# A second recursion level for five of seven block products in a fused layer kernel, with a leftover pass moved ahead

## The chip, the core and the metric

The kernel runs on one core of a Trainium2 chip. The metric is device time in microseconds, the median of several runs. The core has five engines with a queue each, and every queue is worked strictly in order: TensorE (PE, matmuls into the accumulator memory PSUM), VectorE (DVE), ScalarE (ACT), GpSimd (POOL) and SyncE (SP, which here issues all DMAs). An instruction that has to wait for another engine waits on a semaphore, and everything behind it in its own queue waits with it. SBUF is the on-chip working memory; PSUM has eight banks of 512 fp32 columns for each of 128 partitions.

## What is computed

A transformer layer on 2048 tokens of width 512: layer norm, linear attention and a feed-forward network with low-rank expert terms, both added to the input. The part that matters here, cut to its core:

```
gate = x @ W_gate + _lora(x, sA_gate, sB_gate, scale) + _expert_lora(x, A_gate, B_gate, w, scale)
up   = x @ W_up   + _lora(x, sA_up, sB_up, scale)     + _expert_lora(x, A_up, B_up, w, scale)
hidden = jax.nn.silu(gate) * up
out = hidden @ W_down + ...
```

`gate` and `up` have 1376 features each: ten chunks of 128, and 96 left over. All numbers are fp32.

## The kernel before, in words

Tokens are handled in two batches `b` of 1024. After the norm, the normalized input stands transposed in SBUF (`xnT[b]`, two tiles of 256 input features). Features are handled in five pairs `j` of chunks (`j` and `j + 5`), which makes ten *units* (j, b), in the order (0,0), (0,1), (1,0) and so on to (4,1).

In a unit, the product "weights times input" is split into 2x2 blocks: two chunks of features, two blocks of 512 tokens, two halves of the input width. Seven products of block sums (a Strassen scheme in Winograd's form) replace eight. The block sums of tokens are `tsum[b][p]`, those of weights are the eight slots `A11, A12, S1, S3, S2, S4, A21, A22` of a tile for gate and one for up (`wsum[j]`). Each product exists twice (m = 0 for gate, m = 1 for up), and has two matmuls of 512 columns for each: a *wide* product has four matmuls.

Three of the seven products (1, 6 and 5) are done in the units of `unit2` with the same scheme once more: the 2x2 blocks are now gate and up against two halves of the width and two halves of 256 tokens. Such an *inner* product (`inner`, a generator with four steps) has seven matmuls of 256 columns in place of four of 512. It uses one PSUM tile `ab` with two halves `ua` and `lo`, and half of a tile `x` which products 1 and 6 share. ScalarE copies `ua` into the result tiles `r`, VectorE adds `x` and `lo` to them. The inner sums of weights are made by `inner_weight_sums(j)` (VectorE, four instructions of 384 columns for products 1, 5 and 6), those of tokens by `inner_token_sums(b)`. The two units with j = 0 (`unit`) do all seven products wide; `fold`, `attend`, and the inner sums run in between as hooks.

The order on each engine is the order in which the program is written, except on SP. A unit of `unit2` issues: step 1 of product 1; the low-rank terms (`low_rank`, on 64 rows each, gate and up in pairs); half of product 2; then the steps of products 1, 6 and 5 interleaved with the wide matmuls of 2 and 7; then product 3 wide, low-rank terms, product 4 wide. Each of the four output blocks (0,0), (1,1), (0,1), (1,0) is closed by two adds on VectorE and handed to `gated`: Silu on ScalarE, and later (at the next `flush`) a multiplication on VectorE and a store by SP into `h_dram`.

In the b = 0 unit, hooks `mid` and `late` fold a shared low-rank term into the next pair's weights (four small matmuls into four PSUM banks, then four adds on VectorE: `fold_pe`, `fold_adds`), and `end` makes the eight weight sums of the first level (`fold_sums`). In the b = 1 unit, the hook `sums` makes the inner weight sums for the next pair. In the units PSUM has four rotating banks (`bank`) and four held ones (`held`).

The 96 left-over features have their own passes: `rest_weights` loads their weights (and makes a small table on POOL), `fold_rest` adds the shared low-rank term, `rest(b)` does the matmuls for a batch, with Silu, copy, multiplication and a store into `r_dram`. In the kernel before, `rest_weights` stands at j = 2, `fold_rest` in unit (4,0), `rest(0)` between (4,0) and (4,1), and `rest(1)` after (4,1), with the fold of the last down-projection weights in its middle.

Ahead of the units, `query_unit(0)` and `query_unit(1)` make the attention's queries, with hooks for other work; `attend(b, g)` divides them. After the units comes the output stage (`emit_unit`), four blocks of down-projection which read the stored hidden features back (`load_feature`, `feature_sums`). Its tiles come from the slots that the units leave free (`RING`).

Of the kernel before, what the change touches and what calls it, by code (L numbers as in the profile page):

```python
# [9 lines left out]
F32 = mybir.dt.float32  # L10
# [4 lines left out]
P = 128  # L15
# [3 lines left out]
DIV_EPS = 1e-8  # L19

# [15 lines left out]
def layer_kernel(  # L36
# [162 lines left out]
    spread = ffn.tile([P, 2, P], F32, name="spread")  # L199
# [266 lines left out]
    ws = {}  # L466
# [65 lines left out]
    bdiff = ffn.tile([2 * ER, P], F32, name="bdiff")  # L532
# [228 lines left out]
    nc.gpsimd.tensor_sub(bdiff, bgu_sb[:, 0:P], bgu_sb[:, NP * P : (NP + 1) * P])  # L761

    def fold(j, i):
# [5 lines left out]

    query_unit(1, {  # L770
        "P1": [lambda: attend(0, 0)],
        "P5": [lambda: attend(0, 1)],
        "P3": [fold(0, 0)],
    })
    load_weights(1)
    low_rank_in(2)
    low_rank_in(3)
    fold(0, 1)()
    denominators(1)

    def u_tile(name):
        return up_.tile([P, TB], F32, tag="u", name=name)

    def gated(gate, up, m, tag, store):
        h = hp.tile([P, TB], F32, tag="h", name=f"h{tag}")
        nc.scalar.activation(h[0:m, :], gate[0:m, :], AF.Silu)  # L786

        def rest():
            nc.vector.tensor_mul(h[0:m, :], h[0:m, :], up[0:m, :])
            store(h)  # L790

        later(rest)

    def unit(j, b, hooks):

        ws = wsum[j][0]
        tag = f"{j}_{b}"
        f1, f2 = ts(j, P), ts(j + NP, P)
        blk = [ts(0, TB), ts(1, TB)]
        ps = {}  # L800
        c = {}

        def low_rank(terms):
            for p, w, cols, g in terms:
                for m in range(2):
                    ps[m, p] = bank(f"p{p}{m}_{tag}")
                    rows = slice(m * ER, (m + 1) * ER)
                    nc.tensor.matmul(ps[m, p], w[rows, cols], xa[b][rows, blk[g]], start=True, stop=False)

        def products(p):  # L810
            for m in range(2):
                first = (m, p) not in ps
                if first:
                    ps[m, p] = bank(f"p{p}{m}_{tag}")
                for k in range(2):
                    nc.tensor.matmul(  # L816
                        ps[m, p], ws[m][:, A_OF[p], ts(k, P)], tsum[b][p][:, k, :],
                        start=first and k == 0, stop=(k == 1),
                    )
            return ps[0, p], ps[1, p]  # L820

        def gate(half, g):
            def store(h):
                nc.sync.dma_start(
                    out=h_dram[b][j][:, :, 2 * half + g, :].rearrange("s p n -> p s n"),
                    in_=h.rearrange("p (s n) -> p s n", n=UT),
                )

            gated(c[0, half, g], c[1, half, g], P, f"{half}{g}_{tag}", store)

        def hook(name):
            for f in hooks.get(name, ()):
                f()

        low_rank([(2, bgu_sb, f1, 0), (5, bgu_sb, f2, 1)])
        u = [u_tile(f"u{m}_{tag}") for m in range(2)]
        u4 = [u_tile(f"v{m}_{tag}") for m in range(2)]
        pp = products(1)
        for m in range(2):
            nc.scalar.copy(u[m], pp[m])  # L840
        hook("P1")
        pp = products(2)
        for m in range(2):
            c[m, 0, 0] = u_tile(f"c11{m}_{tag}")
            nc.vector.tensor_add(c[m, 0, 0], u[m], pp[m])
        flush()
        gate(0, 0)
        hook("P2")
        pp = products(6)
        for m in range(2):  # L850
            nc.vector.tensor_add(u[m], u[m], pp[m])
        hook("P6")
        pp = products(5)
        for m in range(2):
            nc.vector.tensor_add(u4[m], u[m], pp[m])
        flush()
        hook("P5")
        pp = products(7)
        for m in range(2):
            c[m, 1, 1] = u_tile(f"c22{m}_{tag}")  # L860
            nc.vector.tensor_add(c[m, 1, 1], u4[m], pp[m])
            nc.vector.tensor_add(u[m], u[m], pp[m])
        gate(1, 1)
        hook("P7")
        low_rank([(3, bdiff, f1, 1), (4, bgu_sb, f2, 0)])
        pp = products(3)
        for m in range(2):
            nc.vector.tensor_add(u4[m], u4[m], pp[m])
            c[m, 0, 1] = u4[m]
        flush()  # L870
        gate(0, 1)
        pp = products(4)
        for m in range(2):
            nc.vector.tensor_add(u[m], u[m], pp[m])
            c[m, 1, 0] = u[m]
        flush()
        gate(1, 0)


    TI = {}  # L880
    TH = TB // 2

    def inner_token_sums(b):

        both = slot(7 if b == 0 else 4, [2, 4, TH], f"ti56_{b}")
        if b == 0:
            ti1.append(slot(6, [NBATCH, 4, TH], "ti1"))
        t12 = tsum_pair[b]
        for src, to in ((t12, both), (xnT[b][0][:, :, 0:TB].unsqueeze(1), ti1[0][:, b : b + 1])):
            b11, b12 = src[:, :, 0, 0:TH], src[:, :, 0, TH:TB]  # L890
            b21, b22 = src[:, :, 1, 0:TH], src[:, :, 1, TH:TB]
            nc.vector.tensor_sub(to[:, :, 0], b12, b11)
            nc.vector.tensor_sub(to[:, :, 1], b22, to[:, :, 0])
            nc.vector.tensor_sub(to[:, :, 2], b22, b12)
            nc.vector.tensor_sub(to[:, :, 3], b21, to[:, :, 1])
        for p, t in ((1, ti1[0][:, b]), (5, both[:, 0]), (6, both[:, 1])):
            raw = tsum[b][p]
            TI[b, p] = {1: raw[:, 0, 0:TH], 2: raw[:, 1, 0:TH], 3: raw[:, 1, TH:TB],
                        4: t[:, 3], 5: t[:, 0], 6: t[:, 1], 7: t[:, 2]}

    ti1 = []
    WI = {}

    def inner_weight_sums(j):

        wi = slot(5, [4, 4, P], f"wi{j}")[:, 0:3]
        g, u = (t[:, 0:6:2, :].rearrange("p s (k m) -> p s k m", m=P) for t in wsum[j][0])
        nc.vector.tensor_add(wi[:, :, 0], u[:, :, 0], u[:, :, 1])
        nc.vector.tensor_sub(wi[:, :, 1], wi[:, :, 0], g[:, :, 0])
        nc.vector.tensor_sub(wi[:, :, 2], g[:, :, 0], u[:, :, 0])  # L910
        nc.vector.tensor_sub(wi[:, :, 3], g[:, :, 1], wi[:, :, 1])
        for i, p in enumerate((1, 5, 6)):
            WI[p] = {1: g[:, i, 0], 2: g[:, i, 1], 3: wi[:, i, 3], 4: u[:, i, 1],
                     5: wi[:, i, 0], 6: wi[:, i, 1], 7: wi[:, i, 2]}

    def held(name, k):
        return ps_held[0].tile([P, TB], F32, tag=f"held{k}", name=name)

    def inner(p, b, tag):

        r = [u_tile(f"r{p}{m}_{tag}") for m in range(2)]
        s0, s1 = slice(0, TH), slice(TH, TB)
        ab = bank(f"ab{p}_{tag}", [P, 2, TH])
        ua, lo = ab[:, 0], ab[:, 1]

        def mm(out, n, start=False):
            nc.tensor.matmul(out, WI[p][n], TI[b, p][n], start=start, stop=True, skip_group_check=True)  # L927


        mm(ua, 1, start=True)  # L930
        nc.scalar.copy(r[0][:, s0], ua)  # L931
        x_ = xbank(p, tag)
        mm(x_, 2, start=(p != 6))
        nc.vector.tensor_add(r[0][:, s0], r[0][:, s0], x_)  # L934
        yield r

        mm(lo, 7)
        mm(ua, 6)
        nc.scalar.copy(r[1][:, s0], ua)
        yield r  # L940
        mm(ua, 5)
        nc.scalar.copy(r[1][:, s1], ua)
        nc.vector.tensor_add(r[1][:, s1], r[1][:, s1], lo)
        yield r
        mm(lo, 4)
        mm(ua, 3)
        nc.scalar.copy(r[0][:, s1], ua)  # L947
        nc.vector.tensor_add(r[1][:, s0], r[1][:, s0], lo)  # L948
        yield r

    xs = {}

    def xbank(p, tag):

        if p == 1:
            xs[tag] = bank(f"x_{tag}", [P, 2, TH])
        return xs[tag][:, 1 if p == 6 else 0]

    def unit2(j, b, mid=(), late=(), end=(), sums=()):

        ws = wsum[j][0]
        tag = f"{j}_{b}"
        f1, f2 = ts(j, P), ts(j + NP, P)
        x0, x1 = xa[b][:, 0:TB], xa[b][:, TB:BT]
        c = {}

        def low_rank(terms, start):
            for banks, cols, act in terms:
                for m in range(2):
                    rows = slice(m * ER, (m + 1) * ER)  # L970
                    nc.tensor.matmul(  # L971
                        banks[m], bgu_sb[rows, cols], act[rows, :], start=start, stop=True, skip_group_check=True
                    )
# [483 lines left out]
```

## Time and profile before

| what | value |
|---|---|
| median of 3 runs | 755.51 us (754.02 to 756.65) |
| the profiled run | 756.13 us |
| its span in the profile | 754.3 us |
| mean granted TensorE clock | 1.00 |

Where the stages lie on TensorE, and the busy time of the engines in each (us, read from the profile's table of windows):

| stretch | what | PE | DVE | ACT | POOL |
|---|---|---|---|---|---|
| 221.5 to 283.4 | units (0,0), (0,1) | 61.15 | 47.50 | 8.66 | 3.46 |
| 283.4 to 312.1 | unit (1,0) | 28.67 | 15.19 | 6.14 | 0 |
| 312.1 to 339.1 | unit (1,1) | 27.00 | 18.87 | 6.82 | 0 |
| 339.1 to 478 | units (2,0) to (4,0) | 138.90 | 82.97 | 33.49 | 0 |
| 478 to 492 | `rest(0)` | 14.00 | 3.33 | 3.54 | 0 |
| 492 to 521 | unit (4,1) | 29.00 | 17.10 | 7.91 | 5.87 |
| 521 to 535.5 | `rest(1)` and the last folds | 14.28 | 12.52 | 2.98 | 11.91 |
| 535.5 to the end | output stage | | | | |

The profile is one execution. Its rows show the line, the engine, the operation, the tiles (out<-in), the shape and the count; a timeline row starts with the start time and the length in us, and the bracket at its end is the idle time before it and what ended it. TensorE passes over each fp32 matmul twice, so each matmul of the program shows as two records.

### The profile page before, as it was taken

The numbers are of one execution on the slowest core, as the hardware profiler recorded it, in microseconds if no ns is written. First come the engines' busy times: TensorE is split into PE (matmuls) and PEld (weight loads), VectorE is DVE, ScalarE is ACT, GpSimd is POOL, SyncE is SP. The second block draws the span as 40 slices with busy tenths as digits, with TensorE's granted clock in tenths as the row PEclk, the third lists the DMA queues.
The fourth block names the chain that finished last, engine by engine and source line by source line (L and its number), as shares of the span: only waits on it lengthen the run. The fifth ranks groups of instructions, "written<-read, shape, count | busy, mean of one in ns | idle before, by whom it ended". The sixth has DMA issues, their size and how long they took to land.

```text
span 754.3 us, 8036 instructions
## 1 busy us (share of the span) xinstructions
PE 743.8 (99%) x2950; PEld 467.6 (62%) x2950; DVE 403.7 (54%) x857; ACT 166.5 (22%) x332; POOL 80.7 (11%) x126
## 2 busy tenths in 40 slices
PE   8999999999999999999999999999999999999997
PEld 7666666454343436456456556463688888888886
DVE  5666665455686683774674674439722602603303
ACT  3544442533331112222122122231100000000000
POOL 3111212011000100000000000006601002201001
PEclk9999999999999999999999999999999999999999
DMA  8811001006322212112112122327604407313001
GB/s 223 218 46 43 15 0 57 0 1 167 113 53 70 83 39 77 60 46 67 56 59 73 38 73 77 124 89 204 203 33 175 143 15 234 126 53 115 29 1 56
DMA packets 52729, 63.24 MB, mean 84 GB/s; under 512 B 9426, under 2 KB 39506, under 8 KB 52435
## 3 DMA queue, kind: packets, MB, share of 16 engines
q1 hardware_dynamic: 52018, 62.46, 26.5%
q8 instruction: 23, 0.38, 0.2%
q10 hardware_dynamic: 672, 0.28, 0.2%
q14 instruction: 16, 0.12, 0.1%
HBM read 40.97 MB, written 21.76 MB: 83 GB/s over the span
## 4 chain that ended last, share of the span: by engine, by line
PE 95%; ACT 2%; DVE 2%; issue 0%; DMA 0%; POOL 0%; DVEq 0%; ACTq 0%
PE po L1314 25%; PE ab L927 8%; PE b L977 8%; PE pk L274 7%; PE p L816 7%; PE pg L302 6%; PE x L977 4%; PE p L977 4%; PE pqu L555 3%; PE ph L1337 3%; PE pqv L555 2%; PE pr L1107 2%; PE pxa L634 2%; PE b L971 2%; PE x L927 1%; PE x L971 1%
## 5 line engine op out<-in xcount | busy, mean ns | idle before, releaser
L1314 PE MATMUL po<-wd,f 128*128 128x256 f32 x560 | 122.4, 380 | 0.2 <-DVE xr L1383 0.2
L1314 PEld LDWEIGHTS po<-wd,f 128*128 128x128 f32 x560 | 106.0, 190 | 16.8 <-issue 2.4
L274 PE MATMUL pk<-wk_sb,xnT 128*128 128x256 f32 (+1 forms) x256 | 61.9, 396 | 1.1 <-ACT xnT L262 1.1
L977 PE MATMUL b<-t,w 128*128 128x512 f32 x128 | 61.0, 603 | 0.0
L302 PE MATMUL pg<-kt,xn 128*128 128x512 f32 x128 | 57.5, 592 | 0.0
L274 PEld LDWEIGHTS pk<-wk_sb,xnT 128*128 128x128 f32 x256 | 49.0, 197 | 9.3 <-ACT xnT L262 1.9
L1344 DVE TENSOR_TENSOR had<-ph,wT 64x256 f32<-64x256 f32 x8 | 3.4, 422 | 90.7 <-PE ph L1337 90.6
L1314 PE MATMUL po<-kvo,f 128*128 128x256 f32 x224 | 49.4, 381 | 0.0
L1314 PEld LDWEIGHTS po<-kvo,f 128*128 128x128 f32 x224 | 42.3, 190 | 7.1 <-issue 1.5
L1361 ACT COPY a<-po 128x512 f32<-128x512 f32 x4 | 2.3, 585 | 199.1 <-PE po L1314 159.0
L302 PEld LDWEIGHTS pg<-kt,xn 128*128 128x128 f32 x128 | 24.4, 190 | 25.2 <-issue 23.7
L977 PEld LDWEIGHTS b<-t,w 128*128 128x128 f32 x128 | 23.3, 190 | 25.5 <-issue 24.2
L927 PE MATMUL ab<-ti,wi 128*128 128x256 f32 x144 | 37.6, 379 | 0.0
L927 PEld LDWEIGHTS ab<-ti,wi 128*128 128x128 f32 x144 | 27.0, 190 | 10.9 <-ACT r L931 4.2
L1129 POOL TENSOR_TENSOR wd<-wd 128x256 f32<-128x256 f32 x5 | 3.8, 760 | 269.6 <-issue 267.2
L948 DVE TENSOR_TENSOR r<-r,ab 128x256 f32<-128x256 f32 x24 | 10.1, 419 | 40.3 <-ACT r L947 40.3
L977 PE MATMUL x<-xnT,w 128*128 128x512 f32 x64 | 30.9, 605 | 0.0
L934 DVE TENSOR_TENSOR r<-r,x 128x256 f32<-128x256 f32 x24 | 10.0, 418 | 36.6 <-PE x L927 25.5
L977 PE MATMUL p<-xnT,w 128*128 128x512 f32 x64 | 28.8, 592 | 0.0
L816 PE MATMUL p<-t,w 128*128 128x512 f32 x64 | 28.8, 597 | 0.0
L300 POOL TENSOR_TENSOR ksum<-ksum,kt 128x512 f32<-128x512 f32 x14 | 19.9, 1422 | 78.4 <-DVE kt L292 47.8
L786 ACT ACTIVATE h<-c 128x512 f32<-128x512 f32 x20 | 12.6, 630 | 58.7 <-DVE c L995 29.1
(250 smaller groups left out, 1146.1 us busy)
## 6 DMA issues: line engine op xcount, KB each, us to landing
h_dram<-h SPq DMA_DIRECT2D x40, 256.0 KB
f<-h_dram SPq DMA_DIRECT2D x20, 512.0 KB
x_ring<-in_x_dram SPq DMA_DIRECT2D x16, 256.0 KB
q_dram<-qt SPq DMA_DIRECT2D x16, 256.0 KB
f<-q_dram SPq DMA_DIRECT2D x8, 512.0 KB
xr<-in_x_dram SPq DMA_DIRECT2D x8, 512.0 KB
out_dram<-xr SPq DMA_DIRECT2D x16, 256.0 KB
w<-in_w_gate_dram SPq DMA_DIRECT2D x10, 256.0 KB
```

The source lines that it names most:

```text
L274: nc.tensor.matmul(pk[s], xt(i // TPBATCH, c, cols), wk_sb[:, c, s * HD : (s + 1) * HD + s * E], start=(c == 0), stop=(c == NC - 1),)
L300: nc.gpsimd.tensor_add(ksum, ksum, kt)
L302: nc.tensor.matmul(pg[m], xn[:, ts(m, P)], kt, start=(j == 0), stop=(j == TPBATCH - 1))
L555: nc.tensor.matmul(banks[c], wqs[p][:, k, ts(c, P)], tsum[b][p][:, k, :], start=(start and k == 0), stop=(k == 1), skip_group_check=True,)
L634: nc.tensor.matmul(pa, agu_sb[:, c, :], xt(b, c, cols), start=(c == 0), stop=(c == NC - 1))
L816: nc.tensor.matmul(ps[m, p], ws[m][:, A_OF[p], ts(k, P)], tsum[b][p][:, k, :], start=first and k == 0, stop=(k == 1),)
L927: nc.tensor.matmul(out, WI[p][n], TI[b, p][n], start=start, stop=True, skip_group_check=True)
L971: nc.tensor.matmul(banks[m], bgu_sb[rows, cols], act[rows, :], start=start, stop=True, skip_group_check=True)
L977: nc.tensor.matmul(banks[m], ws[m][:, A_OF[p], ts(k, P)], tsum[b][p][:, k, :], start=start and k == 0, stop=True, skip_group_check=True,)
L1107: nc.tensor.matmul(ps, t[:, k, 0:P], xt(b, k, blk[g]), start=False, stop=(k == NC - 1))
L1314: nc.tensor.matmul(ps[p][:, q, :], lhsT, rhs, start=start, stop=stop, skip_group_check=True)
L1337: nc.tensor.matmul(ph[g * ER : (g + 1) * ER, :], a, f[:, g, :], start=(n == 0), stop=(n == len(chunks) - 1), skip_group_check=True,)
```

## The change

1. All ten units are now of one kind, `unit`, in which five products (1, 2, 6, 5, 3) are inner and only 7 and 4 are wide. The old `unit` is gone, and with it `bdiff`.
2. The order within a unit is new: products 1 and 2 first, then half of 7, the rest of 1, 2, 6 and 5; the first low-rank terms stand after most of 5; then product 3's steps among the ends of 5; the other half of 7; the second low-rank terms; product 4. The results `r` are reused as outputs instead of new tiles `c`.
3. Two of the block additions go to POOL: `r2 += u1` and `r3 += u4` (two 512-column instructions each).
4. `inner_weight_sums` makes sums for products 2 and 3 too: twelve instructions in place of four. Those for 3 overwrite the slot `A21`.
5. The inner token sums are split up: those for 5 and 6 and for 1 on VectorE, those for 2 and 3 on POOL. For b = 0 they are made ahead of the units, for b = 1 within unit (0,0) (hooks `one` and `two`, and POOL's queue).
6. The passes for the left-over features go ahead of the units: loads before `query_unit(1)`, `fold_rest` as its hook, then `low_rank_in`, `denominators`, `rest(0)` with `fold(0, 0)` and `attend(1, 0)` in it, `attend(1, 1)`, `rest(1)` with `fold(0, 1)`.
7. Around the last unit: `fold_down((NP - 1,))` follows the unit directly; feature sums 0, 1, 2 become hooks of unit (4,1).
8. Tiles: `hp` has three buffers for four, `w_rest` takes slot 7, `RING` and the slots of the token sums change, `spread` moves to another pool.

The core of the diff:

```diff
-        i1, i6, i5 = (inner(p, b, tag) for p in (1, 6, 5))
+        i1, i2, i6, i5, i3 = (inner(j, b, p, tag) for p in (1, 2, 6, 5, 3))
         px = [held(f"x{m}_{tag}", m) for m in range(2)]
         pb = [held(f"b{m}_{tag}", 2 + m) for m in range(2)]
         u1 = next(i1)
-        low_rank([(px, f1, x0), (pb, f2, x1)], True)
-        product(2, 0, px)
         next(i1)
-        u2 = next(i6)
+        r2 = next(i2)
+        next(i1)
+        next(i2)
+        product(7, 0, pb, True)
         next(i1)
...
+        add(nc.gpsimd, r2, r2, u1)
         u4 = next(i5)
...
+        low_rank([(px, f1, x0, (True, True)), (pb, f2, x1, (False, True))])
+        next(i6)
+        block(0, 0, r2, r2, px)
+        next(i5)
+        add(nc.vector, u2, u2, u1)
+        run(two)
+        r3 = next(i3)
         flush()
+        next(i3)
+        next(i5)
+        next(i3)
+        add(nc.vector, u4, u4, u2)
         product(7, 1, pb)
+        block(1, 1, u1, u4, pb)
+        next(i3)
+        add(nc.gpsimd, r3, r3, u4)
         run(sums)
...
+    rest(0, (fold(0, 0), lambda: attend(1, 0)))
+    attend(1, 1)
+    token_sums_56(0, slot(6, [2, 4, TH], "ti56_0"))
+    token_sums_1(0)
+    token_sums_23(0, slot(4, [2, 4, TH], "ti23_0"))
+    rest(1, (fold(0, 1), None))
+    flush()
+    inner_weight_sums(0)
```

The new weight sums and the new way in which the hooks are given:

```diff
+        for slots_, ps, to in (
+            (slice(0, 6, 2), (1, 5, 6), [wi[:, 0:3, k] for k in range(4)]),
+            (slice(1, 2), (2,), [wi[:, 3:4, k] for k in range(4)]),
+            (slice(5, 6), (3,), [a21[k // 2][:, :, k % 2] for k in range(4)]),
+        ):
+            g, u = (t[:, slots_] for t in w)
+            nc.vector.tensor_add(to[0], u[:, :, 0], u[:, :, 1])
+            nc.vector.tensor_sub(to[1], to[0], g[:, :, 0])
+            nc.vector.tensor_sub(to[2], g[:, :, 0], u[:, :, 0])
+            nc.vector.tensor_sub(to[3], g[:, :, 1], to[1])
...
+    for j in range(NP - 1):
+        if j > 0:
+            load_weights(j + 1)
+        first = {}
+        if j == 0:
+            first = dict(one=[lambda: token_sums_1(1)], two=[lambda: token_sums_56(1, ti56_1)])
+            token_sums_23(1, slot(7, [2, 4, TH], "ti23_1"))
+        unit(j, 0, [fold_in(j + 1, 0)], [fold_in(j + 1, 1)], [lambda i=i: fold_sums(j + 1, i) for i in range(2)], **first)
+        unit(j, 1, sums=[lambda: inner_weight_sums(j + 1)])
...
+    unit(NP - 1, 1, [lambda: fold_down((0, 2))], [lambda: fold_down((1, 3))],
+         two=[lambda: feature_sums(0, 0)], sums=[lambda: feature_sums(0, 1)], end=[lambda: feature_sums(0, 2)])
     kvo = load_kvo(0)
-    for i in range(2):
-        feature_sums(0, i)
-    for i in range(2, 5):
+    fold_down((NP - 1,), rest=True)
+    for i in range(3, 5):
         load_feature(0, i)
-    rest(1, lambda: fold_down((NP - 1,), rest=True))
```

## The prediction

> **What bounds the kernel now.** First the page: busy times and the chain that ended last.
>
> ```profile
> span 754.3 us, 8036 instructions
> PE 743.8 (99%) x2950; PEld 467.6 (62%) x2950; DVE 403.7 (54%) x857; ACT 166.5 (22%) x332; POOL 80.7 (11%) x126
> PE 95%; ACT 2%; DVE 2%; issue 0%; DMA 0%; POOL 0%; DVEq 0%; ACTq 0%
> ```
>
> TensorE sets the end: every microsecond in which it issues nothing is a microsecond of span. Second, the timeline of TensorE, for the price of the two matmul forms (each matmul of the program shows as two records).
>
> ```profile
> 330.09 3.60 PE L977 MATMUL p<-xnT,w 128*128 128x512 f32 x8
> 318.47 1.46 PE L927 MATMUL ab<-ti,wi 128*128 128x256 f32 x6
> 283.43 0.70 PE L927 MATMUL ab<-xnT,w 128*128 128x256 f32 x2 [0.78 <-DVE u L874]
> ```
>
> A wide record costs (3.60-0.59)/7 = 0.43 us, a narrow one (1.46-0.38)/5 = 0.216 us (0.59 and 0.38: length of one). The third line is the only stall over 0.5 us in the units (283 us, where the first two end).
>
> Third, VectorE in the second half of unit (1,1), which runs from 312.05 to 339.07 us on TensorE.
>
> ```profile
> 328.45 1.29 DVE L1022 TENSOR_TENSOR r<-r,r 128x512 f32<-128x512 f32 x2
> 329.66 0.68 DVE L789 TENSOR_TENSOR h<-h,r 128x512 f32<-128x512 f32 x1
> 330.26 0.69 DVE L789 TENSOR_TENSOR h<-h,c 128x512 f32<-128x512 f32 x1
> 330.86 0.41 DVE L948 TENSOR_TENSOR r<-r,ab 128x256 f32<-128x256 f32 x1
> 331.19 1.28 DVE L1027 TENSOR_TENSOR r<-r,r 128x512 f32<-128x512 f32 x2
> 332.40 1.28 DVE L995 TENSOR_TENSOR c<-r,b 128x512 f32<-128x512 f32 x2
> 333.60 0.55 DVE L908 TENSOR_TENSOR wi<-w 128x384 f32<-128x384 f32 x1
> ```
>
> Here VectorE runs without a break though it is 54% busy on average. Start to start: 0.60 us for 512 columns, 0.34 for 256, about 0.5 for 384 (four weight sums, 333.60 to 335.59). TensorE meanwhile has product 3 (wide, from 330.09): that is what covers the lag. Fourth, the seam between units.
>
> ```profile
> 312.24 1.28 DVE L995 TENSOR_TENSOR r<-r,b 128x512 f32<-128x512 f32 x2
> 313.44 0.42 DVE L724 TENSOR_TENSOR w<-w 128x256 f32<-128x256 f32 x1
> 316.37 0.41 DVE L934 TENSOR_TENSOR r<-r,x 128x256 f32<-128x256 f32 x1
> 312.96 0.63 ACT L786 ACTIVATE h<-r 128x512 f32<-128x512 f32 x1 [3.79 <-DVE r L995]
> 313.50 0.35 ACT L931 COPY r<-ab 128x256 f32<-128x256 f32 x1
> 316.74 1.03 PE L927 MATMUL ab<-ti,wi 128*128 128x256 f32 x4
> ```
>
> The new unit's first copy (L931) queues on ScalarE behind the old unit's last Silu (L786), which waits for the last VectorE block; and the first add of the new unit (316.37) queues behind eight weight sums. VectorE is 4.3 us late here and nobody notices: TensorE has the low-rank terms and half of product 2 to issue (313.00 to 316.7) before it needs either.
>
> **What the change removes on TensorE.** By the order of the built program, 104 wide matmuls go (184 to 80) and 182 narrow ones come (168 to 350): 104 x 2 x 0.43 = 89.2 against 182 x 2 x 0.216 = 78.6, so -10.6 us. The 0.78 us stall and a 0.22 us one before L1105 have no counterpart: -1.0. The 96-feature passes and their weights issue the same TensorE instructions elsewhere: 0 on TensorE. Their 12 loads on SP now stand behind the store of kvo (171.8 us) and are needed near 208 us; hidden. POOL's memset and copies for them hide under that time too; if late, the fold of the rest weights (0.6 us) moves a few matmuls. Sum of gains -11.6.
>
> **What it adds: a walk through a unit.** VectorE gets 15 narrow adds in place of 9, and 12 weight sums in place of 4; POOL gets four 512-column adds (1.27 us each, row of xdiff L1242); the cover is gone, since low rank, product 2 and product 3 no longer stand at the seams. I walk the queues in the built order from zero = the first matmul that waits for ScalarE's first copy, with the spacings above, 0.37 for a copy, 0.54 from Silu to what follows, 0.64 from a narrow matmul's start to its reader, and 0.05 per hand-over.
> TensorE: 21 narrow (9.1) + half of product 7 (1.7) + low rank (2.0) + gaps: product 6's last step at 13.2. Its copy is done at 14.7. Then VectorE: last add of 6 to 15.1; block (0,0) to 16.3; ScalarE gives Silu and only then the next copy, 16.7; add to 17.1; u2 18.3; add 18.6; two gatings 19.8; two adds 20.5; u4 21.7; block (1,1) 22.9; ScalarE puts Silu ahead of the last copy, 23.4; add 23.7. TensorE finished product 3 at 21.9.
> *After a b=1 unit:* twelve sums: four of 0.5 and eight of about 0.22 (128 columns: 0.34 for 256, less the 0.13 by which 384 stand above 256) = 3.8. POOL's two r3 adds start at 23.4 and collide with them. The rows:
>
> ```profile
> 523.66 0.90 POOL L1132 TENSOR_TENSOR wd<-wd 128x256 f32<-128x256 f32 x1
> 523.91 0.94 DVE L1221 TENSOR_TENSOR f<-f 128x256 f32<-128x256 f32 x1
> 528.24 0.41 DVE L1222 TENSOR_TENSOR f<-f 128x256 f32<-128x256 f32 x1
> ```
>
> With two SBUF inputs beside a POOL add, VectorE took 0.94 instead of 0.41; adds from PSUM kept their 0.68. So 2 x 0.5 at least, 2 x 1.27 at most; I take 2.0, as the adds here are twice as wide. Sums end 29.5, gating 30.1, block (0,1) 31.3, gating 32.1; block (1,0) starts 32.1, Silu 32.8, first copy of the next unit done 33.7, TensorE goes on at 33.8. Without stalls a unit is 27.0 - 2 x 0.41 = 26.2. Excess 7.6; I take 7.3, bounds 5.0 (sums at 0.15, collision 1.0) and 8.2. Four times (j = 0..3): 29.2.
> *After a b=0 unit:* the fourth fold matmul needs product 3's bank: 23.9 instead of 22; low rank to 26.4, product 4 and the second fold to 30.8. VectorE: fold adds, gating, block (0,1), four fold adds, gating, block (1,0) to 32.1, eight sums of 0.37 to 35.05, first add of the next unit to 35.5. The next unit's fourth narrow pair, which shares a PSUM tile with that add, would be due 1.4 after its zero: so zero is in effect 34.2 against 27.8 (28.6 measured before, less 0.82). Excess 6.4; I take 6.2, bounds 4.5 and 7. Four times: 24.8.
> *Once each:* `two` of unit (0,0) puts four 1024-column sums (1.2 us each, L434) ahead of all that: 4.6, bounds 4 and 5. The entry into unit (0,0): the weight sums stand behind the last gating of the moved passes (Silu 0.59, copy 0.58, twice, then a gating: 3 us after TensorE ends), third sum 4.5: loss 3.7; POOL's four token sums (5.1) start at the same moment and collide: up to 10.8; I take 7.5. Unit (4,0): no folds or sums after it, still 3.2 (2 to 3.5). Unit (4,1): two feature sums, eight 512-column fold adds and the feature sums at its end now sit on VectorE with 16 POOL differences, and the bank of the second output product waits for the fold add behind them; before, the passes of 521 to 535 us covered that. Walk 12, bounds 6 and 12.6; I take 10.
> Buffers: three h tiles for four, with 9 us or more between reuse; hidden behind stores of 2 to 3 us.
>
> **Sum.** 29.2 + 24.8 + 4.6 + 7.5 + 3.2 + 10 = 79.3, less 11.6 = +67.7. On the profiled span 754.3 that is 822; the median of the runs, 755.5, stands 1.2 above: **823 us**. Low ends: 20 + 18 + 4 + 3.7 + 2 + 6 = 53.7, +42, 797; high ends: 32.8 + 28 + 5 + 10.8 + 3.5 + 12.6 = 92.7, +81, 837.
>
> [...]
>
> [...]
>
> **Rivals.** (a) *The lag is absorbed:* VectorE needs some 20 us a unit of 26, so if block (1,0) starts 0.9 us before a unit's last matmul, no seam stalls and only the gain is left: 755.5 - 11.6 = 744. For it: average load, and a lag of 4.3 at 312 us that cost nothing. Against it: what hid that lag is moved to the middle. Chance 4%. (b) *Less is lost:* POOL's collisions cost little, entry and exit 3.7 and 6, and the second halves overlap better, say 4 a seam: 8 x 4 + 4 + 3.7 + 2 + 6 - 11.6 = +36, 792; 765 to 797. For it: POOL's adds do not touch PSUM adds. 14%. (c) *The idle gaps cost a slower clock:* the first matmuls of the program (18 of 128 columns in 4.10 us, 0.23 each against 0.11 later) show such a state; if each of six gaps brings back half of those 4.1 us at twice the price, 6 x 2 = +12: 835. 10%. (d) Forecast, 797 to 836: 72%.
> Range 790 to 842: the forecast, most of (c) and a part of (b). Within 0.3% is what a measurement here cannot tell from no change (runs lie 754.0 to 756.7): 1%, faster 3%, slower 96%.
>
> **What would show it.** TensorE idle of 4 to 6 us before the third narrow matmul of units (1..4,0), ended by ScalarE's first copy; 2 to 3 us before the second half of the shared x bank in the b=1 units, ended by VectorE; weight sums on VectorE stretched beside POOL; TensorE's share near 90%; narrow records still 0.216 apart. Wrong, if the seams stay closed or VectorE idles while TensorE waits.

## The result, and the profile after

The changed kernel takes 851.88 us (median of 4 runs, 845.6 to 853.05) against 756.08 us before in the same session: 1.125 times as long, interval 1.119 to 1.131. The forecast was 823 us, range 790 to 842: the direction and the places were right, the size was not. The page of the changed kernel, as shown of the kernel before, with the row of the granted clock in 40 equal slices:

```profile
span 851.3 us, 8696 instructions
PE 772.0 (91%) x3106; PEld 510.0 (60%) x3106; DVE 465.7 (55%) x975; ACT 200.6 (24%) x432; POOL 144.4 (17%) x173
PEclk9999999999997999999899899989879999999999
```

Two things add to 97.0 us of span. TensorE stands idle for 851.3 - 772.0 = 79.3 us, where it was 10.5: 68.8 more. And it is busy for 28.2 us longer (743.8 before) although the new matmuls are worth 10.6 us less: 38.8 us of stretched work. The first part was forecast (78.3); the second was not in the sum. The chain that ended last says little here: it can be followed back only to 612.7 us, the end of the units.

The table of windows gives it by stage (the columns after the stretch: its length, then busy time of PE, PEld, DVE, ACT and POOL, granted clock, DMA share, GB/s). The stretches are the end of the queries with the 96-feature passes; the ten units; the output:

```profile
207.00:259.38 52.38, 47.53 (x170) 18.79 (x169) 37.46 (x65) 15.59 (x26) 11.50 (x8) 0.93 0.19 59
259.38:623.93 364.55, 304.70 (x1100) 187.69 (x1100) 224.93 (x461) 94.76 (x239) 61.20 (x52) 0.93 0.18 58
625.07:851.30 226.23, 217.18 (x1089) 180.07 (x1088) 78.36 (x155) 2.97 (x5) 36.14 (x40) 0.98 0.29 97
```

| stretch | before, us | after, us | more |
|---|---|---|---|
| to 207 us | 207.0 | 207.0 | 0 |
| end of the queries and the 96-feature passes (before at 207 to 221.5, 478 to 492, 521 to 535.45) | 42.95 | 52.38 | 9.4 |
| ten units (before 221.5 to 478 and 492 to 521) | 285.5 | 364.55 | 79.05 |
| last folds (before inside the passes) | | 1.14 | 1.1 |
| output stage | 218.85 | 226.23 | 7.4 |

Next the list of TensorE's waits by line and releaser (us in total, times, longest). Before the change its longest entry in the units was 0.8 us:

```profile
PE ab L947 <- ACT r L951: 38.9, 20, 5.0
PE ab L947 <- DVE wi L925: 6.3, 1, 6.3
PE x L947 <- DVE r L953: 5.5, 4, 1.4
PE pf L711 <- DVE r L967: 4.8, 4, 1.4
PE po L1252 <- DVE wd L1103: 4.2, 1, 4.2
PE ab L947 <- ACT ur L818: 2.9, 1, 2.9
...
PE pfr L801 <- ACT qt L565: 1.9, 1, 1.9
```

The first row holds three places: 4.97 us at the four seams after b = 1 units, 0.8 at five seams after b = 0 units, and 1.46 inside every unit. The 1.9, 2.9 and 6.3 us lie ahead of the units and at their entry, the 4.2 us at the exit. The timeline of the seam between units (0,1) and (1,0), all engines, cut to the rows of the chain:

```profile
332.24 2.80 POOL L1006 TENSOR_TENSOR r<-r,r 128x512 f32<-128x512 f32 x2 [11.25 <-ACT r L966]
332.54 1.39 DVE L923 TENSOR_TENSOR wi<-w 128x384 f32<-128x384 f32 x1
333.96 1.51 DVE L924 TENSOR_TENSOR wi<-wi,w 128x384 f32<-128x384 f32 x1
335.39 0.54 DVE L925 TENSOR_TENSOR wi<-w,w 128x384 f32<-128x384 f32 x1
...
338.79 1.28 DVE L1006 TENSOR_TENSOR r<-r,y 128x512 f32<-128x512 f32 x2
340.82 1.28 DVE L1006 TENSOR_TENSOR r<-r,b 128x512 f32<-128x512 f32 x2
341.53 0.63 ACT L863 ACTIVATE h<-r 128x512 f32<-128x512 f32 x1 [1.35 <-DVE r L1006]
342.07 0.35 ACT L951 COPY r<-ab 128x256 f32<-128x256 f32 x1
342.48 1.92 PE L947 MATMUL ab<-xnT,wi 128*128 128x256 f32 x4 [4.97 <-ACT r L951]
```

This is the forecast chain, link by link: two weight sums stretched beside GpSimd's adds, the other sums, block (0,1), block (1,0), Silu, the first copy, TensorE. And the last row shows what the sum left out: four narrow records take 1.92 us where four took 1.03. The clock of the same stretches, from the table of windows:

```profile
342.00:347.00 5.00, 4.52 (x13) 3.71 (x14) 0.94 (x3) 1.54 (x5) 0.00 (x0) 0.66 0.29 95
347.00:366.00 19.00, 17.45 (x71) 11.91 (x69) 9.56 (x21) 6.00 (x16) 2.50 (x2) 1.00 0.05 18
366.00:374.00 8.00, 6.88 (x22) 2.46 (x20) 5.51 (x11) 1.52 (x3) 2.50 (x2) 0.79 0.17 60
```

After the gap of 4.97 us the granted clock is 0.66 over the next 5 us, then 1.00, then 0.79 where a 1.12 us gap falls among matmuls on 8 and 64 rows. A lower clock shows in the records themselves: at a clock of 0.50 narrow records start 0.43 us apart (two of them from 344.19 to 345.04 us) instead of 0.216 ("doubled" below). Cut at the times at which the clock changes, the table of windows shows 0.50 in twelve stretches of the changed kernel, 71.7 us in all, from 8.17:11.58 and 209.56:216.39 to 629.39:636.22. TensorE is busy for 56.2 us of them, and half of that, 28.1 us, is work at full clock that was lost: the larger part of the 38.8.

### The profile page after: what moved, and what is told of

Same layout as the page of the kernel before. It is cut to its first block, busy times and chain, and to the rows that moved or that the text cites. A ratio compares the mean times of both kernels' runs of the same rounds, so it can differ in the third digit from the quotient of the medians.

```text
span 851.3 us, 8696 instructions
## 1 busy us (share of the span) xinstructions
PE 772.0 (91%) x3106; PEld 510.0 (60%) x3106; DVE 465.7 (55%) x975; ACT 200.6 (24%) x432; POOL 144.4 (17%) x173
## 5 line engine op out<-in xcount | busy, mean ns | idle before, releaser
L1006 POOL TENSOR_TENSOR r<-r,r 128x512 f32<-128x512 f32 x40 | 51.8, 1317 | 301.4 <-ACT r L966 301.4
L990 PE MATMUL b<-t,w 128*128 128x512 f32 x160 | 79.1, 623 | 0.0
L967 DVE TENSOR_TENSOR r<-r,ab 128x256 f32<-128x256 f32 x50 | 21.0, 420 | 87.8 <-ACT r L966 87.8
L947 PE MATMUL ab<-xnT,wi 128*128 128x256 f32 x100 | 35.0, 455 | 30.3 <-ACT r L951 23.9
L947 PE MATMUL ab<-ti,w 128*128 128x256 f32 x140 | 40.8, 396 | 17.3 <-ACT r L951 14.6
L863 ACT ACTIVATE h<-r 128x512 f32<-128x512 f32 x40 | 25.2, 630 | 129.5 <-DVE r L1006 80.6
L947 PE MATMUL ab<-ti,wi 128*128 128x256 f32 x180 | 48.6, 388 | 1.1 <-ACT r L951 0.4
L947 PEld LDWEIGHTS ab<-ti,w 128*128 128x128 f32 x140 | 24.7, 189 | 36.7 <-ACT r L951 18.7
L947 PEld LDWEIGHTS ab<-xnT,wi 128*128 128x128 f32 x100 | 22.0, 229 | 37.6 <-ACT r L951 27.6
L303 PEld LDWEIGHTS pg<-kt,xn 128*128 128x128 f32 x128 | 24.4, 190 | 25.2 <-issue 23.6
L947 PE MATMUL ab<-xnT,w 128*128 128x256 f32 x100 | 32.2, 406 | 2.9 <-ACT ur L818 2.9
```

The lines of the kernel that those rows point to most:

```text
L303: nc.tensor.matmul(pg[m], xn[:, ts(m, P)], kt, start=(j == 0), stop=(j == TPBATCH - 1))
L947: nc.tensor.matmul(out, WI[j, p][n], TI[b, p][n], start=start, stop=True, skip_group_check=True)
L990: nc.tensor.matmul(banks[m], ws[m][:, A_OF[p], ts(k, P)], tsum[b][p][:, k, :], start=start and k == 0, stop=True, skip_group_check=True,)
L1006: eng.tensor_add(to[m], t[m], v[m])
```

## The experiments

Twelve kernels ran. The table gives the times, and the length of one pair of units, (1,0) and (1,1), from the first matmul of the one to the first of the unit behind them. Kernels without a range ran once; runs of the changed kernel itself spread over 7 us.

| kernel | us | pair, us |
|---|---|---|
| before | 755.5 | 55.65 |
| changed | 851.9 (845.6 to 853.1) | 71.4 |
| gaps filled (e1) | 835.3 | 68.0 |
| Silu late (e2) | 828.2 | 65.3 |
| sums moved early (e3) | 848.5 | 69.4 |
| rest fold moved (e4) | 850.4 | 70.0 |
| sums spread (e7) | 819.4 | 62.2 |
| e2 and e7 (e5) | 801.3 | 60.9 |
| e5, ends mended (e6) | 799.3 (795.8 to 802.6) | 59.2 |
| e5, fold gap filled (e8) | 805.2 | 59.2 |
| e6, first fold later (e9) | 787.3 (786.4 to 790.0) | 58.7 |
| e9, four inner products (e10) | 798.0 (797.5 to 800.6) | 62.2 |
| changed, adds on VectorE (e11) | 846.1 | 69.0 |
| e10, a wide product as cover (e12) | 776.8 (776.4 to 776.8) | 57.0 |

**e1, is it the gaps that slow the clock?** Matmuls whose result the next one overwrites, in the idle time alone:

```diff
+        for _ in range(extra):
+            nc.tensor.matmul(
+                flat[:, 0:cols], WI[j, 1][1], tsum[b][1][:, 0, 0:cols], start=True, stop=True, skip_group_check=True
+            )
         mm(ua, 1, start=True)
```

> The changed kernel plus matmuls whose results are overwritten, put only where TensorE stands idle: 5 of 512 columns ahead of each b = 0 unit from j = 1 on (7 ahead of unit (0,0)), 3 of 256 ahead of product 3 in the b = 0 units, 2 of 256 in the first fold. About 33 us of extra work on TensorE. Theory G (the gaps make the clock fall, so filling them keeps it up): slow records vanish in the units but not at the exit, which is left alone; 851.9 less 22, 830 us (824 to 838). Theory N (the slow clock belongs to the many narrow matmuls or to traffic beside them, not to the gaps): the slow stretches stay, 852 us or more, up to 885.

Measured 835.25 us: 33 us of useless work made the kernel 16.6 us faster (one run; against the 845.6 to 853.1 of the changed kernel it is 10 to 18). The windows of this kernel, over the same seam and the same fold:

```profile
337.00:342.00 5.00, 4.88 (x19) 3.56 (x20) 1.26 (x3) 1.56 (x5) 0.00 (x0) 1.00 0.22 74
342.00:360.00 18.00, 17.75 (x78) 12.47 (x77) 10.17 (x21) 6.01 (x16) 2.50 (x2) 1.00 0.09 30
360.00:368.00 8.00, 7.94 (x31) 3.41 (x32) 6.25 (x14) 1.14 (x3) 2.49 (x2) 1.00 0.12 38
```

The clock is 1.00 in all three, where it was 0.66 and 0.79. Theory N falls. The exit, left unfilled, kept its 4.4 us gap, and the page of e1 has a clock under 9 tenths in one slice of 40 alone, at 604 to 625 us.

**e2, the Silu that holds up the copy.** Each `gate(...)` is called after the next steps of the inner products:

```diff
         r3 = next(i3)
+        gate(0, 0)
         flush()
...
         block(1, 0, u2, u2, pb)
+        held_gate.append(lambda: gate(1, 0))
```

> The changed kernel with each Silu issued on ScalarE behind the next copies of the inner products instead of ahead of them; the same instructions. Theory S (the Silu that waits for VectorE holds up the copy that TensorE waits for): the gaps of 1.46 us in the ten units shrink to 0.4, those of 1.1 in the folds go, those of 5.0 at the seams shrink by about 1.3; 20 us less idle and some 10 us less at the slow clock: 822 us (810 to 835). Theory V (VectorE alone sets the pace; the copies gain nothing since the next add is late too): each gap reappears at the next matmul that waits for VectorE, 845 to 855 us.

Measured 828.2 us, theory S: the 1.46 us gaps are gone from all ten units. But theory V has a part too, as what waits next appears in the timeline of TensorE:

```profile
306.91 0.70 PE L947 MATMUL x<-xnT,w 128*128 128x256 f32 x2 [2.17 <-DVE r L953]
337.41 1.28 PE L947 MATMUL ab<-xnT,wi 128*128 128x256 f32 x4 [1.86 <-ACT r L951]
```

The seam after the b = 0 unit now waits for VectorE's first add (2.17 us, behind the eight first-level sums), and the one after the b = 1 unit still 1.86.

**e3 and e7, the sums on VectorE.** Both take sums out of the second half of the b = 1 unit. e3 leaves those of product 5 there and puts twelve in a row into the first half:

```diff
-        unit(j, 1, sums=[lambda: inner_weight_sums(j + 1)])
+        unit(j, 1, one=[lambda i=i: fold_sums(j + 1, i) for i in range(2)] + [lambda: sums_of(j + 1, 1)],
+             s2=[lambda: sums_of(j + 1, 3), lambda: sums_of(j + 1, 2)], s6=[lambda: sums_of(j + 1, 6)],
+             sums=[lambda: sums_of(j + 1, 5)])
```

> The changed kernel with the weight sums moved on VectorE: the eight first-level sums from the end of the b = 0 unit and the inner sums of products 1, 2, 3 and 6 from behind block (1,1) into the first half of the b = 1 unit, where VectorE idles; only the sums of product 5 stay in the second half; four more small sums a pair. Theory V (the sums on VectorE make the seams late): the 5.0 us gap at the four seams after b = 1 units falls to 1 or less and the 1.4 us gap early in the b = 1 units goes, 22 us less idle and 8 less at the slow clock: 822 us (812 to 832). Theory S (ScalarE's order is what holds TensorE up): the seams keep 3 us or more, 840 to 850 us.

e3 measured 848.5 us: a miss. Its timeline of TensorE shows why:

```profile
319.94 0.67 PE L959 MATMUL ab<-ti,w 128*128 128x256 f32 x2 [2.69 <-DVE r L974]
345.19 1.13 PE L959 MATMUL ab<-xnT,wi 128*128 128x256 f32 x4 [2.03 <-ACT r L963]
```

The seam shrank from 4.97 to 2.03, and 2.69 us opened in the first half, where an add stands behind the twelve sums. e7 leaves none in the second half and cuts them to fit the idle times of VectorE:

```diff
-        unit(j, 1, sums=[lambda: inner_weight_sums(j + 1)])
+        unit(j, 1, ha=[lambda i=i: fold_sums(j + 1, i) for i in range(2)],
+             hb=[lambda: sums_of(j + 1, 1), lambda: sums_of(j + 1, 3)], hc=[lambda: sums_of(j + 1, 2)])
```

> The changed kernel with the weight sums cut into small groups and put where VectorE idles in its trace: first-level sums behind half of product 7 of the b = 1 unit (3.0 us free there), sums of products 1 and 3 behind the first step of product 6 (2.0 us free), of product 2 ahead of the low-rank terms, of 5 and 6 behind half of product 7 of the next b = 0 unit; none in a second half. ScalarE as in the changed kernel. Theory V (VectorE's sums in the second half make the seam late): the 5.0 us gaps fall to 0.8, as at the seam into unit (4,1) which has no sums before it, and no new gap of over 1 us opens; 821 us (814 to 828). If the earlier move of the sums, which left 2.0 us at the seams and opened 2.6 us in the first half, shows what VectorE can give at most: 845 us.

e7 measured 819.4 us, as theory V had it: the seams after b = 1 units stand at 0.75 us (releaser ACT L965) and no other gap opened. Moving the work was not enough; its pieces had to be shorter than the idle times they went into.

**e5, both.**

> That spreading of the sums together with the late Silus. If the two causes are separate, their savings add: the late Silus gave 24 us, the spread sums some 30 by the last expectation, less what both save at the seams (1.3 us, four times) and the clock that both bring back: 798 us (790 to 806). If one cause stands behind both, no better than the better of the two: 820 us.

Measured 801.3 us. The two causes are separate and their savings add, within the spread of single runs: 851.9 less 23.6 less 32.5 is 795.7. In the units from (1,0) to (4,0) one place with a gap over 0.3 us is left, the first fold. Its windows:

```profile
340.00:351.00 11.00, 9.92 (x42) 5.63 (x38) 8.10 (x17) 3.87 (x9) 1.39 (x2) 1.00 0.15 50
351.00:357.00 6.00, 5.96 (x14) 2.15 (x14) 3.26 (x7) 0.63 (x1) 1.43 (x2) 0.72 0.12 44
```

The gap (0.96 us, at 350.1) is followed by a granted clock of 0.72 over 6 us.

**e8, filling that gap** with two discarded 256-column matmuls (in units (0,0) to (3,0)), nothing else:

```diff
+            if k == NC - 1 and i == 0 and j > 0:
+                for _ in range(2):
+                    nc.tensor.matmul(
+                        pf[2][:, 2 * P :], WI[j - 1, 1][1], tsum[0][1][:, 0, 0:TH], start=True, stop=True,
...
             pf.append(bank(f"pf{i}_{j}_{k}"))
```

> The kernel with late Silus and spread sums (801 us), in whose units one gap of over 0.3 us is left: 0.96 us in the first fold of the b = 0 units from j = 1 on, followed by 3 us of slow records. Here two discarded 256-column matmuls (0.86 us) fill that gap, 8 in all. Theory G (a short gap amid matmuls on 8 and 64 rows is enough to make the clock fall): the slow records of units (1..3,0) vanish, some 3 us each; unit (0,0) has no filling on purpose (its first fold is the one for j = 1, which is filled too), so four times 3: 789 us (786 to 794). If the clock falls for the few rows of these matmuls whatever stands between: 801 us.

As a whole, 805.2 us: no gain, so the expected total is missed. The two executions already differ by 2.8 us when the first unit starts (259.14 against 256.30), where the program is the same: from 200 to 260 us the granted clock is 0.94 in e8 and 0.97 in e5. In the units behind the first pair the reading is clean:

```profile
351.00:360.00 9.00, 8.88 (x37) 4.55 (x35) 9.00 (x20) 2.33 (x6) 2.50 (x2) 1.00 0.18 61
```

Clock 1.00 through the fold, and units (1,0), (2,0) and (3,0) of 30.96 us each, where e5 has 32.59, 32.58 and 30.93. A gap under 1 us thus cost 1.6 us of clock in two units of three, which the totals of the two runs could not have told.

**e6, the ends.** The inner sums of the first unit go ahead of the flush, two folds and two feature sums move:

```diff
+    inner_weight_sums(0)
     flush()
-    inner_weight_sums(0)
...
+    unit(NP - 1, 0, [lambda: fold_down((1,))], [lambda: fold_down((2,))], ha=[lambda: sums_of(NP - 1, 56)])
...
+    unit(NP - 1, 1, [lambda: fold_down((0,))], [lambda: fold_down((3,))],
+         hc=[lambda: feature_sums(0, 0), lambda: feature_sums(0, 1)])
```

> The last one with both ends mended: ahead of the units the inner sums of products 1 and 2 go before the flush and the first-level sums of the up weights; two of the five folds of the down weights go from unit (4,1) to unit (4,0), which has none, and two feature sums go from its second half to the place ahead of its low-rank terms. Theory: 6.3 us at the entry falls to 3, 4.2 us at the exit falls to 1, with the slow clock behind both: 10 us under the kernel before it, 788 us (780 to 798), still slower than before the change, as the pass of the folds of the rest weights (2 us and the slow clock behind it) and the wait for the last bank ahead of the units (2.9 us) are left.

Measured 799.3 us, a miss by 11. The entry's wait fell from 4.7 to 2.5 us and a new one of 2.4 us on VectorE's first add came behind it; at the exit 4.4 fell to 2.0.

**e4 and e9, two folds.** e4 moves the fold of the rest weights:

```diff
-        "P3": [lambda: fold_rest(0), lambda: fold_rest(1)],
...
     denominators(1)
+    for i in range(2):
+        fold_rest(i)
```

> The changed kernel with the fold of the weights of the 96 left-over features moved from ahead of query product 4 to behind the denominators of the second batch. In the changed kernel TensorE waited 1.9 us there for ScalarE to leave the banks and ran 4 us of work at half clock behind it. If that placing is the cause: 847 us (845 to 849) with no gap there. If the wait only moves on: 852 us.

e4: 850.4 us, inside the spread of the changed kernel. The wait moved on: 3.2 us before the first rest pass, and 9.3 us at the entry. e9 leaves this fold in its place with half the banks, and moves the first fold of the units (on top of e6):

```diff
-        run(mid)
         low_rank([(px, f1, x1, (True, True)), (pb, f2, xdiff[b], (False, False))])
         flush()
         block(0, 1, r3, r3, px)
         gate(0, 1)
+        run(mid)
         product(4, 0, pb)
...
+        pf = [bank(f"pfr{k}", [P, 2, P]) for k in range(NC)]
```

> The kernel with both ends mended (799 us), with no filling, but with two orders changed: the first fold stands behind the low-rank terms and the emission of block (0,1), where the bank it waited for is free, and the fold of the rest weights takes four banks in place of eight, which also shifts the rotation so that the first unit no longer begins in the bank of the last rest pass. Theory G: the 0.96 us gaps go with the slow clock behind them (4 us a pair, four pairs), the 1.9 us wait and its slow clock go (4.5 us), the 2.9 us wait shrinks: 799 less 22, 777 us (768 to 784). If the first fold now makes VectorE late for block (0,1): the seams after b = 0 units open again, 790 us or more.

e9: 787.3 us, 1.043 times the kernel before (1.040 to 1.046), 12 under e6 where 22 were expected; the entry's wait grew to 5.0 and the ends kept the rest. With four banks for the rest fold the 1.9 us wait is gone. With the shifted rotation the 2.9 us wait is 0.4, but nothing was won by it: the two waits of the entry are 0.4 + 5.0 here and 2.9 + 2.5 in e6, 5.4 us both times. The pair is 58.7 us with waits over 0.3 us gone:

```profile
352.00:381.00 29.00, 28.73 (x105) 17.66 (x105) 23.11 (x53) 9.82 (x24) 5.46 (x4) 1.00 0.12 40
381.00:411.00 30.00, 29.73 (x119) 18.37 (x118) 19.38 (x43) 9.83 (x24) 5.46 (x4) 1.00 0.24 70
```

TensorE is 99% busy at full clock, and still the pair takes 3.0 us more than before the change, with 1.6 us less to do. Here is a pair of the kernel before, unit by unit:

```profile
312.05:339.07 27.02, 27.02 (x91) 15.27 (x90) 18.92 (x39) 6.79 (x17) 0.00 (x0) 1.00 0.12 41
339.07:367.70 28.63, 28.63 (x108) 15.89 (x107) 15.36 (x32) 6.65 (x16) 0.00 (x0) 1.00 0.25 74
```

The timeline of TensorE in unit (1,1) of e9 shows where the time goes:

```profile
353.12 0.59 PE L967 MATMUL x<-xnT,w 128*128 128x256 f32 x2
353.74 1.13 PE L967 MATMUL ab<-xnT,wi 128*128 128x256 f32 x4
...
356.00 1.03 PE L967 MATMUL ab<-ti,wi 128*128 128x256 f32 x4
...
369.45 1.82 PE L967 MATMUL ab<-ti,w 128*128 128x256 f32 x6
...
375.99 1.50 PE L1005 MATMUL b<-xdiff,bgu_sb 64*128 64x512 f32 x4
```

Two narrow records take 0.43 us from start to start; here the next begins 0.62 us later, 0.19 late, and the four behind the wait take 1.13 instead of 1.03. Five such places (two of them in the row at 369.45, 1.82 where six in a stream take 1.46) cost 1.6 us of the 28.27 us unit. The last row adds 0.5: four low-rank records take 1.50, where the same four took 1.03 before the change (at 334.58). These waits are too short for the profile to name what ended them.

**e10 and e12, a wide product as cover.** Product 3 goes wide again; in e12 half of product 7 also goes ahead of the step that waits:

```diff
-        r3 = next(i3)
...
+        product(7, 1, pb)
         flush()
         next(i5)
         add(nc.vector, u4, u4, u2)
-        product(7, 1, pb)
         block(1, 1, u1, u4, pb)
...
+        for m in range(2):
+            product(3, m, px, True)
```

> The kernel with the moved first fold (787 us) with product 3 wide again, so four inner products in place of five; it accumulates in the bank of block (0,1) as before the change. On TensorE 14 narrow matmuls a unit (6.0 us) give way to 8 wide ones (6.9 us), VectorE loses four adds and the sums of product 3, GpSimd the adds to r3. Theory W (what is left of the loss are many waits of 0.1 to 0.3 us at the narrow steps, about 0.9 us of them in product 3): the units gain nothing or some 0.5 us each although TensorE has 0.8 us more to do: 782 us (775 to 788). If the fifth product pays for itself now that the long waits are gone: 795 us (ten times 0.8 more).

e10: 798.0 us, worse than e9 by 10.8, a miss of theory W. The total is near the 795 of the rival, that the fifth product pays, but not for that reason. Without the steps of product 3 at that place, TensorE came to product 5's last step too early, and a gap of 2.01 us stood in nine units:

```profile
368.47 1.28 DVE L1026 TENSOR_TENSOR r<-r,x 128x512 f32<-128x512 f32 x2
369.67 0.41 DVE L981 TENSOR_TENSOR r<-r,ab 128x256 f32<-128x256 f32 x1
370.14 0.70 PE L966 MATMUL ab<-ti,w 128*128 128x256 f32 x2 [2.01 <-DVE r L981]
```

The add that frees the bank stands behind block (0,0).

> The kernel with four inner products (798 us), with the second half of product 7 (two wide matmuls, 1.7 us) put ahead of the last step of product 5, where that kernel has a gap of 2.0 us in each of nine units that waits for VectorE; and both ends mended further: the fold of the second weight tile goes into the first rest pass, so that the inner sums of the first unit are made ahead of the last pass, and the last fold of the down weights goes ahead of a feature sum. Theory C (a wide product at the place where VectorE is late is what covers the lag; the gaps go if it stands there): ten times 1.8 us less, 6 less at the slow clock, 8 less at the ends: 766 us (758 to 774). If VectorE is only later at the next place: 785 us or more. Theory W says further that a pair of units stays above the 55.6 us of the kernel before, as short waits at the narrow steps are left, so that the whole is no faster than before: over 757 us.

e12: 776.8 us, 1.028 times the kernel before (1.026 to 1.029). Theory C holds in the units: the 2.0 us gaps are 0.3, the pair is 57.04 us, still 1.4 above the kernel before, as theory W says.

```profile
322.83:352.10 29.27, 28.91 (x114) 16.80 (x113) 18.04 (x39) 8.35 (x20) 2.50 (x2) 1.00 0.21 63
352.10:379.87 27.77, 27.42 (x98) 16.26 (x96) 20.96 (x46) 8.34 (x20) 2.50 (x2) 1.00 0.16 50
```

With product 7 as cover, four inner products take 1.6 us a pair less than the five of e9 (58.7); five with the same cover were not tried. The total missed its 766 by a new wait at the entry (timeline, all engines):

```profile
253.98 3.77 DVE L825 TENSOR_TENSOR hr<-hr,ur 32x512 f32<-32x512 f32 x4
255.74 5.17 SPq L826 DMA_DIRECT2D r_dram<-hr  x6
257.45 0.59 ACT L821 ACTIVATE hr<-pr 32x512 f32<-32x512 f32 x1 [11.10 <-DMA r_dram<-hr]
259.88 0.37 ACT L969 COPY r<-ab 128x256 f32<-128x256 f32 x1
260.31 2.07 PE L965 MATMUL ab<-xnT,wi 128*128 128x256 f32 x4 [9.69 <-ACT r L969]
```

The multiplications of the last pass now stood behind sums that ran beside GpSimd's (one took 1.48 us at 252.58); their store freed its tile late, ScalarE waited 11.1 us for the tile, and the first copy behind it. No version here beat the kernel before.

**e11, the two adds back on VectorE:** `add(nc.vector, r2, r2, u1)` and the same for r3.

> The changed kernel with the adds r2 += u1 and r3 += u4 on VectorE in place of GpSimd, and nothing else. Theory V (the second half of a unit is bound by VectorE): r2's add fits into idle time of the first half; r3's adds 1.2 us to the second half and takes away the collision of GpSimd with the weight sums (two sums of 1.4 and 1.5 us instead of 0.55 in the changed kernel's trace, 1.8 us): 0.6 less at each of the four seams after b = 1 units, up to 1.2 more after the others: 855 us (848 to 860). If the collision is what makes the seams late: under 845 us.

Measured 846.1 us, under the expected band, just over the 845 of the rival, and no different from the changed kernel's fastest run (845.6). The four sums of 384 columns take 0.55 us each and the seam is 4.38 us, 0.59 less, as reckoned. The loss after the b = 0 units did not come: 1.12 and 0.83 us as in the changed kernel.

## Why the prediction was right and wrong, by its own steps

The idle time of TensorE by the terms of the sum:

| step | forecast, us | in the trace, us |
|---|---|---|
| after a b = 1 unit, four times | 7.3 | 4.97 at the seam + 1.46 inside the unit = 6.4 |
| after a b = 0 unit, four times | 6.2 | 0.83 + 1.38 + 1.12 (1.41 in the first) + 1.46 = 4.8 |
| `two` in unit (0,0) | 4.6 | 1.4 |
| entry into unit (0,0) | 7.5 | 2.92 + 6.32 = 9.2 |
| after unit (4,0) | 3.2 | 0.76 + 1.46 = 2.2 |
| unit (4,1) and exit | 10 | 1.46 + 0.90 + 0.98 + 4.17 = 7.5 |
| fold of the rest weights | 0 | 1.9 |

The sum in the trace is 67, against 79.3 forecast. The walk had the mechanism, the places and the releasers: 4 to 6 us before the third narrow matmul of units (1..4,0), ended by ScalarE's first copy, is 4.97 four times. "2 to 3 us before the second half of the shared x bank" is 1.38, ended by VectorE as said. The sums beside GpSimd took 0.84 and 0.96 us longer, 1.8 where 2.0 were taken. In the rows such a sum ends shortly after the add beside it: GpSimd's second add ends at 332.24 + 2.80 = 335.04, the sum that began beside it at 333.96 ends at 335.47, 0.43 later. In the prediction's row the add ended at 523.66 + 0.90 = 524.56, the sum at 524.85, 0.29 later. Neither of the two sums at the seam lost the 1.27 us of a whole add, which the walk took as the upper bound.

**The step that failed** is the price of TensorE's own work: "104 x 2 x 0.43 = 89.2 against 182 x 2 x 0.216 = 78.6, so -10.6 us", and the sign named for it, "narrow records still 0.216 apart". (104 x 2 x 0.43 is 89.4, a slip of 0.2 that changes nothing.) Both prices are those of a full clock and of matmuls that never wait. In a stream at full clock they held: six narrow records take 1.46 us after the change as before. But busy time rose by 28.2 us instead of falling by 10.6, 38.8 us of stretch in all. Of this the slow clock is 28.1 us by the trace, the half of 56.2 us at a clock of 0.50. It stood only in rival (c), at 12 us and 10%, for six gaps. It came after more than the six: the folds' gaps near 1 us brought it too (0.79 and 0.72), the 1.9 us wait of the rest fold and the exit.

e1 shows by experiment that the gaps bring it: with most of them filled the kernel gained 16.6 us. It does not give back all 28.1, as the ends were left unfilled (a mean clock of 0.992 over the span of 833.5 us is still some 13 us at 0.50) and as TensorE at full clock reaches the next wait sooner.

The other 10.7 us are what is left for short waits and restarts. In the changed kernel they were not measured one by one; e9, with full clock and no wait over 0.3 us in the pair, shows their kind: at the narrow steps they cost 1.6 us a unit, twice the 0.8 us that the two further products save.

The total then comes out of two errors of opposite sign: 823, plus 38.8 of stretch, less the 9.5 us by which the idle time was forecast too high (78.3 more, measured 68.8), is 852.

Gaps of very different length had the slow clock behind them: 4.97 us at the seams (a clock of 0.66 over 5 us), 2.01 us in e10 (two narrow records take 1.19 us behind the gap that ends at 399.63 us, 0.70 behind another), and in the folds 1.12 us in the changed kernel and 0.96 us in e5 (0.79 over 8 us, 0.72 over 6). In the kernel before, where the longest gap of the units is 0.78 us, the clock is 1.00.

**"The moved passes 0 on TensorE"** held for their work but not for the place: the stretch is 9.4 us longer. Of this 2.9 us is the wait for the last bank, which the entry's term covers, and 1.9 us with the slow clock behind it is the fold of the rest weights, which was costed at 0.6 us "if late". Eight banks asked for at once, among banks that ScalarE was still reading: e9 took four, and the wait was gone.

**The rivals.** (a) fell: no seam closed by itself. (b) had its point (less idle than forecast) and was outweighed. (c) was the right addition to the forecast, and the two should have been summed: 823 + 12 = 835. Its size was too small by more than half, 12 against the 28.1 of the trace, as it counted six gaps and the folds brought the slow clock too.

## What to carry to other kernels

When an edit makes TensorE wait, reckon with a slow clock behind the waits beside the idle time (here 28.1 us beside 68.8), and look among matmuls on few rows first, where a gap of 1.0 to 1.1 us was enough in four of the six folds of units (1,0) to (3,0) in the changed kernel and e5. Price shorter matmuls with their waits: here a step that waits for a copy cost 0.1 us in restart and 0.2 to 0.3 us in hand-over even where no gap shows, and that ate the whole gain of these products. Sums and activations that are not urgent go behind the copies that TensorE waits for, in pieces shorter than the idle time they use, and a wide matmul belongs where the other engines are late.

## What was not expected of the hardware

- Discarded work made the kernel faster: 33 us of it, 16.6 us gained.
- The same gap does not always bring the slow clock. In e10 nine units have one of 2.01 us at the same step. Behind the one that ends at 399.63 us the next two narrow records take 1.19 us and a wide record is 1.06 long, where 0.59 is its length at full clock; behind the one that ends at 370.14 us two narrow ones take 0.70 and three wide ones 1.45. In the changed kernel none of the ten gaps of 1.46 or 1.47 us among matmuls on 128 rows has a slow clock in the 7 us behind it. Of the three gaps of 1.12 us in the folds, two have it, 1.9 and 2.0 us after their end (368.06 and 439.66 us), and the third, which ends at 511.30 us, has not.
- The times at which the clock changes are evenly spaced in the changed kernel's trace. Its twelve stretches at 0.50 are 3.41, 6.83 or 10.24 us long, wherever the gaps are, and each begins and ends a whole number of 3.413 us steps from the first, to 0.02 of a step: from 8.17 to 342.68, 441.66 and 636.22 us it is 98, 127 and 184 (628.05 / 184 = 3.413). Three rows of the table of windows, the first and the third of one step each, the second of seven:

```profile
342.68:346.09 3.41, 3.41 (x9) 2.70 (x9) 0.20 (x1) 0.74 (x2) 0.00 (x0) 0.50 0.20 70
346.09:369.98 23.89, 21.22 (x89) 14.01 (x89) 13.60 (x29) 7.26 (x19) 4.84 (x4) 1.00 0.07 23
369.98:373.40 3.42, 3.42 (x7) 1.17 (x4) 1.89 (x3) 0.63 (x1) 0.15 (x1) 0.50 0.22 79
```

- Filling 0.86 of a 0.96 us gap was enough: in e8 the clock is 1.00 from 351 to 368 us, where e5 has 0.72 from 351 to 357.
